# Two expert tiles computed during the second image's routing, a check moved into attention's tail, and the mambas' opening reordered

## The chip, the cores and the metric

The kernel runs on one core of a Trainium2 chip, in fp32 throughout. A core has engines with instruction streams of their own that synchronise by semaphores: TensorE (PE; its weight loads are shown as PEld), VectorE (DVE), ScalarE (ACT), GpSimd (POOL) and SyncE (SP). SP, ACT and POOL also issue DMAs. Each engine runs its instructions in the order in which they were written. The metric is the device time of one execution in microseconds (us), lower is better.

## The reference, cut to what matters

Four layers run over x of shape (2, 128, 56, 56): two images, 128 channels. Each layer adds its output to x, and each reads x after a group norm (32 groups per image).

```python
x = x + _L0(_gn(x))   # agent attention
x = x + _L1(_gn(x))   # 3x3 convolution
x = x + _L2(_gn(x))   # patch experts
x = x + _L3(_gn(x))   # two mambas, forward and backward, fused, layer norm

# layer 2: a token is a 2x2 patch of all channels: 2*784 = 1568 tokens of 512
logits = xp @ router_w                       # (1568, 8)
topv, topi = top_k(softmax(logits), 2); topv = topv / sum(topv)
for e in range(8):
    val, g = split(xp @ w1[e], 2)            # w1[e]: (512, 2048)
    out += gate[:, e:e+1] * ((val * sigmoid(g)) @ w2[e])   # w2[e]: (1024, 512)

# layer 3, for each row of the image (56 steps long)
xc = silu(conv_b + causal conv of 4 taps of (x @ in_w.T))
dt, B, C = split(xc @ xproj_w.T); dt = softplus(dt @ dt_w.T + dt_b)
h = exp(dt * A) * h + (dt * xc) * B          # 16 states per channel, scanned
y = (sum over states of h * C + xc * D) * silu(z)
```

The norm of an image needs the whole image, so a layer of image b can begin only when the layer before has ended for image b. The two images are independent of each other up to that.

## The kernel before

**Attention and the convolution.** Attention ends with a list `tail` of small stages that are put one by one before the pieces of the convolution of image 0 (`parts`, each a left or right half of the four groups of rows `GROUPS`). After the last group a check follows (L854 to L872): maxima and minima of attention's sums are compared with limits, and PE adds the findings of all partitions into `w_ps`, from which `wide` is set. `wide` chooses after this program whether a slower variant must run. Only then come the planes of image 1's convolution (L135, L947) and that convolution itself, the loop `conv(1)`, which yields after each group.

**Routing (`PatchExperts.route`).** `patches(b)` normalises image b into xq, computes the logits (l_ps, s_ps), takes the two best experts per token on DVE (L1122 to L1131), transposes the tokens (xt_ps, copied by ACT into one of four xt buffers) and writes them to DRAM (xd, seven DMAs of 224 KB on SP). `patches(0)` runs during `conv(1)`, `patches(1)` after it. Then, once for both images: the shares (L1156 to L1160, with an Exp on ACT), counts per expert (tot and pre on PE, a scan on DVE), the number of 128-slot tiles of each expert, the expert of each tile (`whose`), each token's slot, and 28 matmuls into `inv` (L1267) that turn "slot of each token" into "token and share of each slot". `whom` and `share` are copied from it (L1276, L1278). The scheduler also puts the preparation of the mambas' weights (`MambaWeights`: transposes tr_ps, copies L142, scalings L1471) into this stretch.

**Experts (`PatchExperts.run`).** At least 25 tiles (`fewest`) and up to 7 more in a Switch; 28 were run. For a tile j: SP loads w1 (4096 KB) and w2 (2048 KB) of the expert into one of two buffers each; POOL gathers the tile's 128 rows from xd (xr, an indirect DMA); `up` transposes them (xr_ps), DVE copies them (xs_c), 16 matmuls of 512 columns (each two records) give h_ps, ACT takes the sigmoid and DVE the product he; `down` of the tile before transposes he (he_ps) and multiplies by w2 (o_ps), scales by the share and writes to DRAM (os). Tile 0 waits for the gather, this for `whom`.

**The mambas' opening (`mamba_pair`).** `arrive(b)` is a generator that brings image b back: for each of seven pieces k0 to k6, POOL gathers two rows per token from os (g), DVE adds them, PE transposes the sum into y_ps, DVE adds it to x and takes statistics; last comes the norm (gn_ps twice, `ir_v`). `arrive(0)` runs alone. `arrive(1)` is called `second`, and runs in pieces beside the first block of image 0: an agenda of steps (conv, silu, low, step, error, log, softplus, weigh, send_steps, ...) is written out by hand, and after each step a number from a tuple says how many pieces of `second` are pulled. Every engine then keeps this order (`manual_schedule`). `send_steps` (L1795) copies dt and dt*u to the layout with two states per partition: for the first block per half m, eight DMAs of 112 KB for dtu on SP and eight for dt on ACT. After the opening the main loop begins: `decay` (L1807, exp on ACT), `push` (L1818, dBu on POOL), `scan` (L1840 on DVE), and the products with C (L1849 on DVE for most, L1846 on POOL for some), for which PE spreads C into c_ps (L1828).

Of the kernel before, what the change touches and what calls it, by code (L numbers as in the profile page):

```python
# [8 lines left out]
F32 = mybir.dt.float32  # L9
# [8 lines left out]
P = 128  # L18
# [390 lines left out]
def short_attention(net, wide, conv):  # L409
# [20 lines left out]
    with ExitStack() as ctx:  # L430
# [337 lines left out]
        with tc.manual_schedule(engines={E.PE, E.Activation, E.DVE}):  # L768
# [55 lines left out]
            for f in fetches:  # L824
                if f:
                    f()

# [7 lines left out]
                [deviations],  # L835
# [15 lines left out]


            bad = net.small.tile([P, 4], F32, name="bad", tag="bad")
            nc.vector.memset(bad, 0.0)  # L854
            worst = net.small.tile([P, 4], F32, name="worst", tag="worst")
            aflat = asum.rearrange("t b k h -> t (b k h)")
            for n, (v, op, cmp, limit) in enumerate(
                (
                    (ends[:, 0].rearrange("p b k -> p (b k)"), ALU.max, ALU.is_gt, 1e20),
                    (ends[:, 1].rearrange("p b k -> p (b k)"), ALU.min, ALU.is_lt, 1e-30),  # L860
                    (aflat, ALU.max, ALU.is_gt, 1e30),
                    (aflat, ALU.min, ALU.is_lt, 1e-20),
                )
            ):
                size = v.shape[0]
                nc.vector.tensor_reduce(worst[:size, n : n + 1], v, AX.X, op)
                nc.vector.tensor_single_scalar(bad[:size, n : n + 1], worst[:size, n : n + 1], limit, cmp)
            total = net.small.tile([P, 1], F32, name="bad_sum", tag="bad_sum")
            nc.vector.tensor_reduce(total, bad, AX.X, ALU.add)
            w_ps = bank("w_ps")  # L870
            nc.tensor.matmul(w_ps[0:1, 0:1], full[:, 0:1], total, start=True, stop=True)
            nc.vector.tensor_single_scalar(wide, w_ps[0:1, 0:1], 0.5, ALU.is_gt)  # L872
# [130 lines left out]
TILES = 32  # L1003


class PatchExperts:

# [14 lines left out]
    def route(self, dram, wpool, conv):  # L1022
# [9 lines left out]
        with tc.tile_pool(name="l2_route", bufs=1) as one, tc.tile_pool(  # L1032
            name="l2_route_ps", bufs=2, space=PSUM
        ) as ps:
            self.fewest = -(-2 * toks // SLOTS)
            none = one.tile([SLOTS, 512], F32, name="none")
# [38 lines left out]
            nc.gpsimd.tensor_scalar(floor, count_to[:, :most], float(SLOTS), 0.0, ALU.mult, ALU.add)  # L1075

# [5 lines left out]
            per = nt // NB  # L1082

            def patches(b):
                if b == 0:
                    self.xq = wpool.tile([P, 4, 2 * self.hidden], F32, name="xq", tag="w1")
                xq = self.xq
                mr = net.group_norm(b, ps, "tr")
                for q in range(4):
                    net.normed(  # L1090
                        xq[:, q, b * tok : (b + 1) * tok].rearrange("c (h w) -> c h w", w=half), self.place(b, q), mr
                    )
                lq = one.tile([P, tok], F32, name="lq", tag="lq")
                size = tok // 2
                for i in range(2):
                    l_ps = ps.tile([P, 512], F32, name="l_ps", tag="tr")
                    for q in range(4):
                        nc.tensor.matmul(
                            l_ps[32 * q : 32 * q + 32, :size],
                            rw[:, q, :],  # L1100
                            xq[:, q, b * tok + i * size : b * tok + (i + 1) * size],
                            start=True,
                            stop=True,
                        )
                    nc.scalar.copy(lq[:, i * size : (i + 1) * size], l_ps[:, :size])
                s_ps = ps.tile([P, 512], F32, name="s_ps", tag="tr")
# [16 lines left out]
                for n in range(2):  # L1123
# [6 lines left out]
                    if n == 0:  # L1130
# [7 lines left out]
                        )  # L1138
                for t in range(b * per, (b + 1) * per):
                    tp = ps.tile([P, 512], F32, name="xt_ps", tag="tr")  # L1140
                    for q in range(4):
                        nc.tensor.transpose(tp[:T, q * P : (q + 1) * P], xq[:, q, t * T : (t + 1) * T], net.ident)
                    xt = one.tile([T, 512], F32, name="xt", tag="xt", bufs=4)
                    nc.scalar.copy(xt, tp[:T, :])
                    nc.sync.dma_start(self.xd[t * T : (t + 1) * T, :], xt)

            for _ in conv(0):
                pass
            for k, _ in enumerate(conv(1)):
                if k == 0:  # L1150
                    patches(0)
            patches(1)


            share = [one.tile([T, nt], F32, name=f"share{n}") for n in range(2)]
            nc.vector.tensor_sub(share[1], tops[1], tops[0])  # L1156
            nc.scalar.activation(share[1], share[1], AF.Exp)
            nc.vector.tensor_scalar_add(share[0], share[1], 1.0)
            nc.vector.reciprocal(share[0], share[0])
            nc.vector.tensor_mul(share[1], share[1], share[0])  # L1160


            both = one.tile(shape, F32, name="both")
            nc.vector.tensor_add(both, hots[0], hots[1])
            flat = both.rearrange("t n e -> t (n e)")
            tot = ps.tile([P, 512], F32, name="tot", tag="tr")
            nc.tensor.matmul(tot[:, : nt * experts], every, flat, start=True, stop=True)
            pre = ps.tile([P, 512], F32, name="pre", tag="tr")
            nc.tensor.matmul(pre[:T, : nt * experts], before, flat, start=True, stop=True)
            by_e = one.tile([P, experts, nt], F32, name="by_e")  # L1170
            nc.vector.tensor_copy(by_e, tot[:, : nt * experts].rearrange("p (n e) -> p e n", e=experts))
            upto = one.tile([P, experts, nt], F32, name="upto")
            nc.vector.tensor_tensor_scan(
                upto.rearrange("p e n -> p (e n)"),
                step.rearrange("p e n -> p (e n)"),
                by_e.rearrange("p e n -> p (e n)"),
                0.0,
                ALU.mult,
                ALU.add,
            )  # L1180

            over = one.tile([P, experts, most], F32, name="over")
            nc.vector.tensor_tensor(
                over,
                upto[:, :, nt - 1 : nt].to_broadcast([P, experts, most]),
                floor.unsqueeze(1).to_broadcast([P, experts, most]),
                ALU.is_gt,
            )
            tiles = one.tile([P, experts], F32, name="tiles")
            nc.vector.tensor_reduce(tiles, over, AX.X, ALU.add)  # L1190
            ends = one.tile([P, experts], F32, name="ends")
            nc.vector.tensor_tensor_scan(ends, every_e(net, one, experts), tiles, 0.0, ALU.mult, ALU.add)

            more = keep.tile([1, 1], I32, name="more")
            nc.vector.tensor_scalar_add(more, ends[0:1, experts - 1 : experts], -float(self.fewest))
            self.more = more
# [933 lines left out]
```

## Time and profile before

| | |
|---|---|
| median of three runs | 3127.28 us (3126.38 to 3134.36) |
| the profiled execution | 3131.49 us |
| its span in the trace | 3129.8 us |
| mean granted TensorE clock | 0.931 |
| busy: PE, DVE, ACT, POOL | 2836.3, 2229.0, 1758.0, 1495.6 us |
| attention's scores (L617) | 40.1 to 888.4 us |
| convolutions (L971), from | 894.5 us |
| routing's end (whom, L1276) | 1023.5 us |
| experts' last output (L1353) | 1678.9 us |
| first scan of the mambas (L1840) | 1757.1 us |
| w1, w2: issue to landing (median) | 19.4, 10.2 us |

A line of a timeline gives the start in us from the span's start, the length, engine, line, operation, output and inputs with their shapes and the number of instructions merged, and in brackets the engine's idle time before it with what ended it. An fp32 matmul leaves two records. "ACTq" and "SPq" are DMA issues.

### The profile page before, as it was taken

What the parts mean: (1) busy time and instruction counts of PE and PEld (TensorE: products, weight loads), DVE (VectorE), ACT (ScalarE), POOL (GpSimd) and SP (SyncE); (2) the same over time, 40 slices, a digit from 0 to 9 for tenths busy, and PEclk for the clock granted to TensorE, in tenths of its full rate; (3) what the DMA queues carried; (4) which work ended last, traced back from release to release, by engine and by line L of the source; (5) the groups of instructions that cost most, each with busy time, mean ns of one, the idle gap of its engine ahead of it and who ended that gap; (6) DMA issues with size and microseconds to landing.
All of it is one profiled execution on the core that took longest, in us unless ns stands there. A gap on an engine that the chain in (4) does not pass through costs nothing. (4 is left out here: it accounts for less than half of the span.)

```text
span 3129.8 us, 34601 instructions
## 1 busy us (share of the span) xinstructions
PE 2836.3 (91%) x12964; PEld 1082.0 (35%) x12964; DVE 2229.0 (71%) x2033; ACT 1758.0 (56%) x2634; POOL 1495.6 (48%) x793
## 2 busy tenths in 40 slices
PE   7999999999988899999996789989899899899885
PEld 3333333332335444444443223333223333233321
DVE  5879999998886011111112689999999999999996
ACT  5778888887741011111110577776777776777764
POOL 3000100100521000000002589999999999999996
PEclk9999999999998899999997789999889998899987
DMA  1000000000011777777854553444434535444440
GB/s 54 1 1 1 1 1 1 1 1 1 1 38 53 311 308 302 301 310 292 319 194 161 104 110 77 93 92 102 90 84 86 114 81 107 90 85 91 93 101 8
DMA packets 133525, 333.64 MB, mean 107 GB/s; under 512 B 20228, under 2 KB 90724, under 8 KB 129748
## 3 DMA queue, kind: packets, MB, share of 16 engines
q1 hardware_dynamic: 111104, 303.96, 33.8%
q0 software_dynamic: 5136, 14.70, 1.4%
q10 hardware_dynamic: 17092, 12.53, 1.3%
q8 instruction: 106, 1.74, 0.2%
q14 instruction: 87, 0.71, 0.1%
HBM read 262.56 MB, written 17.20 MB: 89 GB/s over the span
## 5 line engine op out<-in xcount | busy, mean ns | idle before, releaser
L1818 POOL TENSOR_TENSOR dBu<-dtu,Bs 128x896 f32<-128x896 f32 x448 | 944.9, 2142 | 54.9 <-DVE h L1840 45.4
L1840 DVE TENSOR_TENSOR_SCAN h<-dA,dBu 128x896 f32<-128x896 f32 x448 | 879.1, 2007 | 51.3 <-ACT dA L1807 49.2
L620 ACT ACTIVATE ex<-sc 128x896 f32<-128x896 f32 (+1 forms) x700 | 602.6, 917 | 125.1 <-PE sc L617 113.8
L627 DVE TENSOR_TENSOR ex_sum<-ex_sum,ex 128x1792 f32<-128x1792 f32 (+1 forms) x238 | 492.5, 2069 | 35.3 <-ACT ex L620 21.3
L1860 PE MATMUL y<-h,both 128*64 128x448 f32 x1792 | 477.3, 635 | 13.7 <-POOL h L1846 12.6
L617 PE MATMUL sc<-q,k 32*128 32x448 f32 (+1 forms) x2800 | 403.8, 588 | 3.6 <-ACT ex L620 2.9
L1330 PE MATMUL h_ps<-w,xs_c 128*128 128x512 f32 x896 | 392.7, 596 | 11.8 <-issue 9.9
L1807 ACT ACTIVATE dA<-dt,f_A 128x448 f32<-128x448 f32 x448 | 284.4, 637 | 104.8 <-DVE h L1840 76.6
L635 PE MATMUL av<-ex,va 128*32 128x448 f32 (+1 forms) x2800 | 334.4, 552 | 0.1
L1849 DVE TENSOR_TENSOR h<-h,c_ps 128x1792 f32<-128x1792 f32 x154 | 311.3, 2022 | 26.8 <-PE c_ps L1828 12.3
L1334 DVE TENSOR_TENSOR he<-h_ps,sg 128x512 f32<-128x512 f32 x56 | 38.6, 691 | 397.7 <-PE h_ps L1330 374.9
L582 POOL TENSOR_TENSOR a_e<-a_e,a_inv 112x784 f32<-112x784 f32 x14 | 41.6, 2973 | 584.2 <-ACT ex L620 394.6
L1807 ACT ACTIVATE dA<-dt,b_A 128x448 f32<-128x448 f32 x448 | 283.7, 636 | 62.0 <-DVE h L1840 49.8
L1281 POOL DMA_INDIRECT xr<-xd,whom x28 | 28.0, 999 | 534.7 <-PE xr_ps L1320 494.7
L1846 POOL TENSOR_TENSOR h<-h,Cs 128x1792 f32<-128x1792 f32 x70 | 279.3, 3990 | 5.9 <-DVE h L1840 5.9
L1828 PE MATMUL c_ps<-low,ident 40*64 40x448 f32 x616 | 172.3, 640 | 91.5 <-DVE h L1849 69.3
L1330 PEld LDWEIGHTS h_ps<-w,xs_c 128*128 128x128 f32 x896 | 168.7, 191 | 220.3 <-issue 202.4
L1860 PEld LDWEIGHTS y<-h,both 128*64 128x64 f32 x1792 | 118.3, 152 | 320.6 <-issue 258.5
L617 PEld LDWEIGHTS sc<-q,k 32*128 32x128 f32 (+1 forms) x2800 | 137.9, 181 | 230.1 <-issue 132.5
L1351 PE MATMUL o_ps<-w,ht 128*128 128x512 f32 x448 | 198.7, 596 | 7.9 <-DMA w<-in_L_conv_w_dram 7.9
L1353 ACT ACTIVATE ot<-o_ps,share 128x512 f32<-128x512 f32 x28 | 19.2, 687 | 285.7 <-PE o_ps L1351 285.7
L1333 ACT ACTIVATE sg<-h_ps 128x512 f32<-128x512 f32 x56 | 33.4, 597 | 257.9 <-PE h_ps L1330 257.9
(333 smaller groups left out, 3067.5 us busy)
## 6 DMA issues: line engine op xcount, KB each, us to landing
w<-in_L_conv_w_dram SPq DMA_DIRECT2D x28, 4096.0 KB, 19.4
w<-in_L_conv_w_dram SPq DMA_DIRECT2D x28, 2048.0 KB, 10.2
Bs<-far SPq DMA_DIRECT2D x56, 896.0 KB, 10.7
dtu<-sp_u SPq DMA_DIRECT2D x108, 224.0 KB, 3.9
dt<-dt SPq DMA_DIRECT2D x108, 224.0 KB, 5.2
Cs<-far SPq DMA_DIRECT2D x140, 112.0 KB, 7.4
os<-ot ACTq DMA_DIRECT2D x28, 256.0 KB, 7.7
xd<-xt SPq DMA_DIRECT2D x14, 224.0 KB, 2.7
```

The lines of the kernel that those rows point to most:

```text
L617: nc.tensor.matmul(sc[:size, j, :BLK], self.m.k[rows, at : at + size], self.q[rows, :], start=True, stop=True)
L620: nc.scalar.activation(ex[:size, 2 * g : 2 * g + 2, :], sc[:size, :, :BLK], AF.Exp, scale=scale)
L627: nc.vector.tensor_add(self.total[g][:size], self.total[g][:size], ex[:size])
L635: nc.tensor.matmul(self.av[rows, :BLK], self.m.va[:size, i, rows], self.ex[i][:size, h, :], start=i == 0, stop=i == STEPS - 1,)
L1330: nc.tensor.matmul(h_ps, xc[:, q, :], w1[:, q, f0 : f0 + 512], start=q == 0, stop=q == 3)
L1351: nc.tensor.matmul(o_ps, ht[:, i, :], w2[:, i, :], start=i == 0, stop=i == nj - 1)
L1807: nc.scalar.activation(self.dA[u][:, r * BLK : (r + 1) * BLK], self.dt2[:, m, r, :], AF.Exp, scale=self.w.A[:, j, 2 * m + r : 2 * m + r + 1],)
L1818: nc.gpsimd.tensor_tensor(self.dBu[u], self.dtu2[:, m], self.B[:, j, :].unsqueeze(1).to_broadcast(shape), ALU.mult)
L1840: nc.vector.tensor_tensor_scan(hf, af, bf, 0.0, ALU.mult, ALU.add)
L1846: nc.gpsimd.tensor_tensor(h4, h4, c, ALU.mult)
L1849: nc.vector.tensor_tensor(h4, h4, c, ALU.mult)
L1860: nc.tensor.matmul(self.y[r * H : (r + 1) * H, m, :BLK], both, self.hc[j][:, m, r, :], start=False, stop=j == PAIRS - 1)
```

## The change

1. The check's DVE instructions become `judge`, its matmul `verdict`, and both are put into attention's tail.
2. `EARLY = 2` tiles are taken ahead. After `patches(0)`, `first_tiles` finds two tiles that are full with image 0's tokens (a copy of the routing for seven token groups, with 14 matmuls of four columns into inv_0), and `ahead` issues their weights and gathers. A tile's work is cut into stages (turn; four times four products; of the tile before: turn and two halves of o_ps). `patches(1)` and the rest of the routing are written in a fixed order for PE and ACT, with `go(n)` putting the next n stages in between: thirteen in all, those are both tiles' `up` and tile 0's `down`. Tile 0's sigmoids are held until the shares' Exp is done. The routing of all tokens counts the full tiles of image 0 first and the rest after, so that every tile of the first kind keeps its number. xq holds one image at a time (`room`), xt has two buffers instead of four; `inv` is built in four halves that share `room` with xq. The mambas' weights are prepared after the routing, and kept in the same `room`.
3. In the opening the tuple is another, and dt's eight DMAs of the first block are issued by POOL instead of ACT. In the order that results, dt's issues stand ahead of the last two pieces' gathers (k5, k6) on POOL, and the norm of image 1 and its two matmuls ahead of the backward conv on PE.

```diff
+            def judge():
+                bad = net.small.tile([P, 4], F32, name="bad", tag="bad")
...
+                nc.vector.tensor_reduce(total, bad, AX.X, ALU.add)
+                judged.append(total)
+            def verdict():
+                w_ps = bank("w_ps")
+                nc.tensor.matmul(w_ps[0:1, 0:1], full[:, 0:1], judged[0], start=True, stop=True)
+                nc.vector.tensor_single_scalar(wide, w_ps[0:1, 0:1], 0.5, ALU.is_gt)
...
-                [deviations],
+                [deviations, judge],
+                [],
+                [verdict],
...
             def patches(b):
-                if b == 0:
-                    self.xq = wpool.tile([P, 4, 2 * self.hidden], F32, name="xq", tag="w1")
+                go = self.go if b == 1 else lambda n: None
+                got = []
+                go(2)
+                for stage in net.norm_stages(b, ps, "o", got.append):
+                    fetch = stage()
+                    if fetch:
+                        fetch()
+                        go(1)
...
+                go(1)
+                s_ps = ps.tile([P, 512], F32, name="s_ps", tag="o")
...
+                shares(some)
+                if b == 1:
+                    held, self.held = self.held, None
+                    for stage in held:
+                        stage()
                 for t in range(b * per, (b + 1) * per):
...
-                    xt = one.tile([T, 512], F32, name="xt", tag="xt", bufs=4)
+                    xt = one.tile([T, 512], F32, name="xt", tag="xt", bufs=2)
                     nc.scalar.copy(xt, tp[:T, :])
                     nc.sync.dma_start(self.xd[t * T : (t + 1) * T, :], xt)
+                    if t % 4 == 1:
+                        go(1)
...
+            def first_tiles():
+                some = slice(0, per)
...
+                pre = counted(both, by_e, upto, steps)
...
+                nc.vector.tensor_scalar_min(self.whose_0, whose, float(experts - 1))
...
+                inv = ps.tile([P, 512], F32, name="inv_0", tag="o")
+                for n in range(2):
+                    hot = one.tile(here, F32, name="hot_0", tag="hot_0")
+                    nc.vector.tensor_copy(hot, hots[n][:, some, :])
+                    split(hot, slot, some, at)
+                    lq = one.tile([P, small_room], F32, name="lq", tag="lq")
+                    turned(inv[:, : 2 * EARLY], lq, n, some, EARLY, n == 0, n == 1)
+                self.whom_0 = keep.tile([P, EARLY], I32, name="whom_0")
+                nc.vector.tensor_copy(self.whom_0, inv[:, :EARLY])
...
                 if k == 0:
                     patches(0)
-            patches(1)
+                    first_tiles()
+                    self.ahead()
+            with tc.manual_schedule(engines={mybir.EngineType.PE, mybir.EngineType.Activation}):
+                patches(1)
...
+                pre = counted(both, by_e, upto, step)
...
+                self.go(2)
...
+                for n in range(2):
+                    at_n = one.tile([T, nt], F32, name=f"at{n}")
+                    split(hots[n], slot, slice(0, nt), at_n)
...
+                    for b in range(NB):
+                        self.go(1 if self.stages else 0)
+                        turned(
                             inv[:, : 2 * TILES],
+                            room[:, b * size : (b + 1) * size],
...
+        def ahead():
+            self.stages, self.held = [], []
+            for j in range(EARLY):
+                e = expert(j)
+                self.stages += step(j, e, up_weights(e), gather(j))
+    def later(self, stage):
+        if self.held is None:
+            stage()
+        else:
+            self.held.append(stage)
+    def go(self, n):
+        for _ in range(n):
+            self.stages.pop(0)()
...
-        for j in range(self.fewest):
+        for j in range(EARLY, self.fewest):
             e = expert(j)
-            w1, w2 = up_weights(e), down_weights(e)
...
+            tile(j, e, up_weights(e), gather(j))
...
+        room = one.tile([P, N], F32, name="weights", tag="room")
...
-                for to, src, queue in ((self.dtu2, self.dtu, nc.sync), (self.dt2, self.dt, nc.sync if m is None else nc.scalar)):
+                for to, src, queue in ((self.dtu2, self.dtu, nc.sync), (self.dt2, self.dt, nc.sync if m is None else nc.gpsimd)):
...
-                for _ in range((0, 0, 0, 0, 2, 1, 2, 1, 2, 0, 0, 0, 0, 0, 1, 1, 1)[step - first] if step - first < 17 else 1):
+                for _ in range((0, 0, 0, 2, 0, 0, 1, 0, 0, 1, 1, 0, 3, 1, 1, 1)[step - first] if step - first < 16 else 1):
                     next(second, None)
...
-                    experts.route(dram, wpool, convolved)
-                    wts = MambaWeights(net, one, nat, bank)
...
+                    experts.begin(wpool, work, ps)
+                    room = one.tile([P, 4 * experts.tok], F32, name="room", tag="room")
+                    experts.route(dram, work, ps, room, convolved)
+                    with tc.tile_pool(name="l3_nat", bufs=2) as nat:
+                        wts = MambaWeights(net, one, nat, bank)
+                    experts.run()
```

## The prediction

> **What bounds the kernel now.** I read the page's 40 slices first. TensorE (PE) is at 9 or 8 tenths in most slices; the change works in two places where it is not: around 30% (the experts' start) and 54 to 57% of the span (the mambas' opening). The windows of the experts' start follow; columns: stretch, its length, busy time of PE, PEld, DVE, ACT, POOL, then granted clock, DMA share, GB/s.
>
> ```profile
> 983.00:1011.00 28.00, 18.30 (x101) 11.99 (x100) 23.90 (x104) 5.94 (x14) 1.31 (x2) 0.81 0.18 59
> 1011.00:1024.00 13.00, 12.18 (x56) 12.02 (x56) 4.27 (x10) 0.00 (x0) 0.04 (x1) 0.50 0.71 283
> 1024.00:1034.76 10.76, 1.99 (x8) 1.62 (x9) 0.69 (x1) 0.00 (x0) 5.09 (x5) 0.50 1.03 388
> 1034.76:1073.70 38.94, 38.13 (x98) 17.38 (x97) 4.84 (x7) 5.02 (x8) 1.55 (x2) 0.96 0.67 271
> ```
>
> From 983 to 1034.76 PE does small work and waits; two tiles' products (38.9 us) come after that. PE's timeline of it (start, length, idle time before in brackets):
>
> ```profile
> 935.45 0.19 PE L871 MATMUL w_ps<-bad_sum,full 128*1 128x1 f32 x2 [5.63 <-DVE bad_sum L869]
> ...
> 969.07 13.73 PE L971 MATMUL conv_ps<-planes,cwt 128*128 128x448 f32 x48
> ...
> 991.16 3.60 PE L1098 MATMUL l_ps<-xq,rw 128*32 128x392 f32 x16
> ...
> 1011.26 12.18 PE L1267 MATMUL inv<-room 112*128 112x64 f32 x56 [5.18 <-DVE tile_f L1242]
> 1031.36 1.09 PE L1320 MATMUL xr_ps<-ident,xr 128*128 128x128 f32 x4 [7.92 <-DMA xr<-xd,whom]
> ...
> 1034.76 15.55 PE L1330 MATMUL h_ps<-w,xs_c 128*128 128x512 f32 x32
> ...
> 1053.38 13.90 PE L1330 MATMUL h_ps<-w,xs_c 128*128 128x512 f32 x32
> 1067.11 5.31 PE L1351 MATMUL o_ps<-w,ht 128*128 128x512 f32 x12
> ...
> 1073.70 13.97 PE L1330 MATMUL h_ps<-w,xs_c 128*128 128x512 f32 x32 [0.39 <-issue]
> ```
>
> The third tile's products start at 1073.70 and one tile then takes 22.54 us (1073.70 to 1096.24): whatever start the third tile has is handed on to the end. For the opening, the timelines of DVE, ACT and PE:
>
> ```profile
> 1756.07 0.16 DVE L66 TENSOR_SCALAR ir_v<-gn_ps 128x1 f32<-128x1 f32 x1 [7.38 <-PE gn_ps L116]
> 1757.09 2.02 DVE L1840 TENSOR_TENSOR_SCAN h<-dA,dBu 128x896 f32<-128x896 f32 x1 [0.86 <-ACT dA L1807]
> ...
> 1769.32 2.02 DVE L1849 TENSOR_TENSOR h<-h,c_ps 128x1792 f32<-128x1792 f32 x1
> ```
> ```profile
> 1743.51 2.55 ACTq L1795 DMA_DIRECT2D dt<-dt  x4
> 1746.10 0.53 ACT L1773 COPY dt<-sp_ps 128x448 f32<-128x448 f32 x1 [3.46 <-issue]
> ```
> ```profile
> 1747.90 8.01 PE L1690 MATMUL conv_ps<-pad,b_conv_t 128*128 128x448 f32 x16
> ...
> 1766.61 1.76 PE L1828 MATMUL c_ps<-low,ident 40*64 40x448 f32 x4
> ```
>
> The first scan waits for the second image's norm (`ir_v`), and that for `gn_ps`, which PE runs behind the backward conv's 8.01 us. The first product with C (L1849) starts as c_ps (1766.61) and the fourth scan end together.
>
> **Part 1, the check (`judge`).** Its ten DVE instructions and `w_ps` stand between the last statistics (932.87) and the next planes (L135, 935.92). Beside attention's tail they cost nothing as long as the conv's matmuls cover them (PE busy 29.82 of 900 to 933); without cover 1.85 us, their sum. Gain 2.4 us (0.5 to 2.4).
>
> **Part 2, two tiles ahead.** I work out when the third tile's products can start. Conv(1) ended at 982.8. It starts 2.4 earlier, and takes on tot and pre (0.45 each before), 14 `inv` matmuls of four columns (nearest row: 14 records of s_ps, seven matmuls, in 1.45 at clock 0.97, so 0.2 each: 2.9), and about 1 us of waits, since xt has two buffers and an xd takes 2.7 to land (0 to 3): end 985.2. Then the list of tokens (0.2), the gather's issue (1.0) and landing, with 6 MB of weights in flight behind it: xr's rows give 2.7 (xd, idle queue) to 7.4 (the first gather, at DMA share 1.03). I take 991.5. On POOL the two gathers, which wait for that list, stand ahead of conv(1)'s last sums (L991/L992), so image 1's statistics come at about 988; SP has the xd copies of image 0 ahead of w1, which costs nothing while those land by 973. PE runs in its written order, so image 1's norm and routing stand behind tile 0's gather and w1:
> - tile 0 and 1: xr and its copy 2.0 and 0.6, products 15.4 and 13.7;
> - norm 0.9, l_ps 3.6, s_ps 1.6, seven xt 3.7, tot and pre 0.9;
> - 28 `inv`: the row is 12.18, at clock 0.50; s_ps at clock 0.97 is 0.207 a matmul, so 5.8. Now 512-column products lie between the groups, as from 1034.76 on, where the clock was 0.96: I take 6.1 (5.8 to 12.2);
> - down(0): he 1.2, o_ps 7.0.
>
> Sum 56.7. The Trainium skill, "TensorE: Matmul & The Clock Gate", Part 1, says that the clock is halved by default and released by some 3.4 us of sustained work; here PE was busy for 12.18 of 13 us and the clock stayed 0.50, so the rule alone would not have given the row. By the rule the sum is as above; if `inv` cannot raise the clock, as in the row, it is 6.1 us worse.
>
> Idle time inside: the Exp of the shares, a table load (1.28 us in the opening) and two sigmoids (0.6 each) come ahead of the xt copies on ACT, behind twelve DVE selections of 0.2: xt waits 4.5; two xt buffers instead of four make PE wait for two landings (0.58 + 0.3 + 2.7 each, less 3.2 of work): 4; tot for `both`: 1. Together 9.5 (3 to 15). `inv` ends at 1057.7, whom at 1058.1, the gather (1.0, landing 7.3 to 8.0) at 1066.3, xr and he to products 1.4: 1067.7. Left is the mambas' weights: 34 copies and 16 scalings of 0.28 on DVE, 14 us which before lay beside the routing (983 to 1007). Now they start at 1058; the gather's wait hides 8, and transposes between tile 2's products cost PE 3 to 6. Effective start 1072.5 against 1073.70. **Gain 1.2, judge included** (from a gain of 9: few stalls and a quick gather, to a loss of 7: `inv` at half clock, as many stalls).
>
> The steady tiles and the Switch keep their instructions; the number of tiles does not grow, since each full tile taken early is one less later.
>
> **Part 3, the opening.** dt's eight copies go from ACT to POOL. ACT's copy of sp_ps (m = 1) no longer stands behind four issues: 1746.10 becomes about 1744.3 (PE's last sp_ps ends there), and with fewer y_ps pieces between, up to 5 earlier. But POOL then has, in order: memset, four issues, memset, four issues, and only then the gathers of the last two patch tiles (k5, k6), which before had been issued by 1729.5. POOL's direct issues at the program's start took 0.53 to 0.82; at 0.65 and a first memset at 1738 to 1743.4, the issues end by 1743.5 to 1748.8. The last of four gathers (one each 1.28) begins 3.8 later and lands after 3.4 (median of `g`). Add 0.9, y_ps 1.3, additions 1.0, statistics 0.7, aggregate to `ir_v` 2.0: 5.9. So `ir_v` at 1756.6 to 1761.9 against 1756.07, and the first scan 0.5 to 5.8 late. PE's backward conv (8.0, now after `gn_ps`) ends at 1764.5 to 1769.8 instead of 1755.9; xc, table load and silu 2.9, low 3.2, its copy 0.5, gate 1.9, c_ps 1.8: first L1849 at 1775 to 1780, 6 to 11 late. Waited on behind it are DVE's next scans and ACT's dt for the backward half. DVE's idle time up to 1810 (1.09, 2.84, 4.77, 1.24, 1.87, 2.63) could absorb some; it hangs on the same chain, so I let 6 through. **Loss 6 us** (0 to 11; a gain of 3 if POOL is quick, since dBu's first product ends at 1752.7 and only `ir_v` held the first scan back).
>
> The Trainium skill, "DMA: Bandwidth & Descriptors", Specifications, gives the GpSimd path a first byte at about 1 us and the sync/scalar path 0.6, a rule against this move; ACT's rows here are 4.0 us to landing, POOL's for plain copies are not shown. By the rule the sum would be 0.4 worse.
>
> **Sum.** -1.2 + 6 = +4.8 on the profiled execution, 3131.49 (span 3129.8 and 1.7 around it): 3136.3. That run lies 4.2 above the median of the runs, 3127.28; against that: **3132**.
>
> **Rivals.**
> - *The opening absorbs its delay, and the routing's stalls are small* (faster). For: DVE idles 14.4 us just behind the first L1849; ACT is freed of 5.2 us of issues. Against: those waits name ACT's dt and PE's c_ps. Experts -9, opening -3: 3115. Chance 0.17.
> - *POOL's queue decides the opening* (slower). POOL runs dBu and the gathers in order; if its issues take 0.8 and its gathers land late (5.4 at most before), L1849 is 11 late and all of it is kept; with the xt stalls at their upper end (+4 to +7) 3143. It decides from 9.4 us in sum. For: POOL's dBu is already what follows. Chance 0.28.
> - *The early tiles do not run early*: w1 lands late (19.4 us is the median to landing, in steady state) and image 1's norm stands behind it on PE. Landing at 995 rather than 990 costs 4: 3136. Inside the forecast's range.
>
> **How the numbers follow.** Forecast (little change) 0.55, faster 0.17, slower 0.28. A measurement of this kernel can tell about 0.3% (9.4 us) from no change, so these are also the three chances. The likeliest case alone spans 3123 to 3137; the bounds together -9 to +18; leaving a tenth out on either side, 3119 to 3143.
>
> **What would show it.** `w_ps` gone from before the planes; tile 0's h_ps near 993; `inv` in four groups, ending at 1057 and at a clock near 0.95; h_ps of the third tile between 1068 and 1077 with tr_ps among it; gathers g of k5 and k6 behind dt's issues on POOL; `ir_v` at 1757 or later and L1849 6 or more behind its place relative to the end of the experts. I am wrong if the experts' gain exceeds 10, if the first L1849 is not late, or if the tiles' 22.54 us has changed.

## The result, and the profile after

| | before | after |
|---|---|---|
| median, lowest and highest of 14 runs each | 3127.32 us (3122.20 to 3134.36) | 3137.48 us (3132.06 to 3148.23) |
| profiled execution, its span | 3131.49, 3129.8 us | 3145.05, 3143.3 us |
| mean granted clock | 0.931 | 0.927 |

The ratio after to before is 1.0035, with a 95% interval of 1.0023 to 1.0047: slower by 10.2 us, just beyond the 0.3% that can be told from no change. The forecast was 3132 us with a range of 3119 to 3143. The range held the time; the likeliest case, 3123 to 3137, did not. The two profiled executions lie 4.2 and 7.6 us above the medians of their kernels, so the traces differ by more than the medians do.

I compared the two traces at the same events. Each time is the start of the instruction, and the last row is the end of the span:

| event | before | after minus before |
|---|---|---|
| attention's last score | 888.8 us | +1.4 |
| first matmul of the convolutions | 894.5 | +2.1 |
| first matmul of conv(1) | 938.5 | +2.1 |
| first products of the fourth tile | 1096.2 | +1.6 |
| experts' last o_ps | 1678.3 | +1.1 |
| opening's pad | 1710.9 | +1.2 |
| first scan | 1757.1 | +6.7 |
| fifth scan | 1773.0 | +13.3 |
| last scan | 3100.8 | +12.7 |
| end | 3129.8 | +13.6 |

The first 2.1 us arise before the convolutions, in code that the change leaves alone: in the traces of this case the first matmul of the convolutions starts anywhere from 892.7 to 899.5 us. From there to the experts' end the change gains about 1 us (2.1 becomes 1.1); the opening costs 12.2 us, from pad to fifth scan, and of that 11.5 are left at the last scan.

Three timelines of the kernel after show the opening, of POOL, DVE and PE in this order; the columns are those of the timelines before.

```profile
1736.76 0.11 POOL L1984 MEMSET dt<- 128x8 f32 x1 [12.08 <-DVE sp_u L1980]
1737.31 2.16 POOL L1995 DMA_DIRECT2D dt<-dt  x4 [0.43 <-POOL dt L1984]
1739.49 0.11 POOL L1984 MEMSET dt<- 128x8 f32 x1
1739.99 2.06 POOL L1995 DMA_DIRECT2D dt<-dt  x4 [0.40 <-POOL dt L1984]
1745.16 1.04 POOL L1419 DMA_INDIRECT g<-os,at_i  x1 [3.11 <-DMA dt<-dt]
...
1749.12 0.99 POOL L1419 DMA_INDIRECT g<-os,at_i  x1 [0.31 <-issue]
```
```profile
1752.57 2.23 DVE L1601 TENSOR_TENSOR g<-g,g 112x512 f32<-112x512 f32 x1 [13.14 <-DMA g<-os,at_i]
...
1762.79 0.16 DVE L66 TENSOR_SCALAR ir_v<-gn_ps 128x1 f32<-128x1 f32 x1 [0.74 <-PE gn_ps L116]
1763.81 2.02 DVE L2040 TENSOR_TENSOR_SCAN h<-dA,dBu 128x896 f32<-128x896 f32 x1 [0.86 <-ACT dA L2007]
...
1779.42 2.02 DVE L2040 TENSOR_TENSOR_SCAN h<-dA,dBu 128x896 f32<-128x896 f32 x1 [7.20 <-ACT dA L2007]
1781.76 2.02 DVE L2049 TENSOR_TENSOR h<-h,c_ps 128x1792 f32<-128x1792 f32 x1 [0.32 <-PE c_ps L2028]
```
```profile
1754.94 0.99 PE L1604 MATMUL y_ps<-ident,g 112*128 112x112 f32 x4 [16.74 <-DVE g L1601]
...
1762.61 9.07 PE L1890 MATMUL conv_ps<-pad,weights 128*128 128x448 f32 x16
...
1779.96 1.76 PE L2028 MATMUL c_ps<-low,ident 40*64 40x448 f32 x4
```

In the kernel before, POOL had issued all gathers ahead of its first memset, which waited for DVE:

```profile
1724.55 0.98 POOL L1281 DMA_INDIRECT g<-os,at_i  x1 [0.30 <-PE y_ps L1408]
...
1728.50 0.98 POOL L1281 DMA_INDIRECT g<-os,at_i  x1 [0.30 <-issue]
1743.36 0.11 POOL L1784 MEMSET dt<- 128x8 f32 x1 [13.89 <-DVE sp_u L1780]
```

In the change POOL's four gathers of the last two pieces stand behind both memsets on dt and eight issues. DVE waits 13.14 us for them and PE 16.74. The norm of image 1 follows, and only behind its matmuls PE runs the backward conv, which before began at 1747.90 and now at 1762.61. What follows from that conv is late: ACT's silu (L1899, L2071), the fourth scan's dA behind it on ACT (DVE waits 7.20), c_ps and the first product with C (1769.32 before, 1781.76 now).

In the experts, PE's timeline of the kernel after answers to the one shown of before:

```profile
931.66 0.19 PE L852 MATMUL w_ps<-bad_sum,full 128*1 128x1 f32 x2 [0.91 <-DVE bad_sum L847]
932.28 2.51 PE L979 MATMUL conv_ps<-planes,cwt 128*128 128x224 f32 x12 [0.43 <-DVE x L996]
...
996.10 1.12 PE L1465 MATMUL xr_ps<-ident,xr 128*128 128x128 f32 x4 [5.31 <-DMA xr<-xd,whom]
...
1023.99 1.10 PE L1168 MATMUL xt_ps<-ident,room 128*112 128x128 f32 x4 [4.53 <-ACT xt L1170]
...
1056.95 1.67 PE L1246 MATMUL inv<-room 112*128 112x64 f32 x14
...
1066.45 0.69 PE L1465 MATMUL xr_ps<-ident,xr 128*128 128x128 f32 x2 [4.31 <-DMA xr<-xd,whom]
...
1073.76 1.12 PE L1475 MATMUL h_ps<-w,xs_c 128*128 128x512 f32 x2 [0.27 <-DVE xs_c L1467]
```

PE now has products to do from 998 on, where before it ran the routing and waited, from 1011 to 1034 us at half clock. But the gather of the third tile can only be issued when `inv` ends at 1058.6. PE has a few small transposes for that time (tr_ps) and then waits 4.31 us; behind xr_ps more transposes for the mambas' weights come, 7.3 us until the first product, and others between the third tile's products. The fourth tile starts at 1097.88 against 1096.24.

### The profile page after: what moved, and what is told of

It reads as the page before. It is cut to its first block, busy times and chain, and to the rows that moved or that the text cites. A ratio compares the mean times of both kernels' runs of the same rounds, so it can differ in the third digit from the quotient of the medians.

```text
span 3143.3 us, 34651 instructions
## 1 busy us (share of the span) xinstructions
PE 2842.2 (90%) x12996; PEld 1080.0 (34%) x12996; DVE 2246.2 (71%) x2096; ACT 1758.2 (56%) x2635; POOL 1500.0 (48%) x804
## 5 line engine op out<-in xcount | busy, mean ns | idle before, releaser
L2060 PE MATMUL y<-h,weights 128*64 128x448 f32 x1792 | 476.4, 633 | 12.2 <-POOL h L2046 11.2
L1475 PE MATMUL h_ps<-w,xs_c 128*128 128x512 f32 x896 | 395.9, 598 | 10.9 <-issue 10.3
L2049 DVE TENSOR_TENSOR h<-h,c_ps 128x1792 f32<-128x1792 f32 x154 | 311.3, 2021 | 28.0 <-PE c_ps L2028 13.6
L2060 PEld LDWEIGHTS y<-h,weights 128*64 128x64 f32 x1792 | 118.1, 152 | 320.9 <-issue 257.7
L1890 PE MATMUL conv_ps<-pad,weights 128*128 128x448 f32 x448 | 186.0, 563 | 3.6 <-ACT pad L1797 2.4
## 6 DMA issues: line engine op xcount, KB each, us to landing
w<-in_L_conv_w_dram SPq DMA_DIRECT2D x28, 2048.0 KB, 10.2
Cs<-far SPq DMA_DIRECT2D x140, 112.0 KB, 10.3
```

The costliest lines, as they stand in the source:

```text
L1475: nc.tensor.matmul(has["h"][:, n, :], has["xc"][:, q, :], w1[:, q, f0 : f0 + 512], start=q == 0, stop=q == 3)
L2049: nc.vector.tensor_tensor(h4, h4, c, ALU.mult)
L2060: nc.tensor.matmul(self.y[r * H : (r + 1) * H, m, :BLK], both, self.hc[j][:, m, r, :], start=False, stop=j == PAIRS - 1)
```

## The experiments

Medians are over the runs of each, with the ratio to before measured on the same chip and its 95% interval. The ratio is not that of the two medians: in before_again, the same code on both sides, the medians differ by 2.8 us and the ratio is 1.0001. Traces are compared over the stretch that a change touches, since single executions of one kernel differ by some microseconds elsewhere.

**opening_undone**: the change with the old opening, so its experts and its check alone.

```diff
-  ... nc.sync if m is None else nc.gpsimd
+  ... nc.sync if m is None else nc.scalar
-  (0, 0, 0, 2, 0, 0, 1, 0, 0, 1, 1, 0, 3, 1, 1, 1)[step - first] if step - first < 16 else 1
+  (0, 0, 0, 0, 2, 1, 2, 1, 2, 0, 0, 0, 0, 0, 1, 1, 1)[step - first] if step - first < 17 else 1
```

> The changed kernel with the opening of before (the old tuple, dt's copies on ACT). Theory (the opening alone loses 12.6 us, the experts and the check together gain 1.4, the 2.1 us up to attention's end is noise): ratio to before 0.9995, some 3126 us; third tile within 1 us of where it is in the changed kernel relative to attention's end, first L1849-kind product 12 us after the first scan as before. Rival (the new pools, the shared weights room or the experts' order also slow the mambas or the experts): at least half of the loss stays, 3132 us or more.

Measured: 3129.45 us, ratio 1.0019 (1.0009 to 1.0028). In the trace the first convolution to the last o_ps is 0.1 us shorter than before, and pad to fifth scan 0.7 shorter. So the loss of 12.2 sits in the opening. The median's 5 us over before (3124.15 in this set of runs) is found in no stage up to the fifth scan; I come back to it below.

**queue_back**: the change with dt's eight issues on ACT again, the new tuple kept.

```diff
-  ... nc.sync if m is None else nc.gpsimd
+  ... nc.sync if m is None else nc.scalar
```

> The changed kernel with dt's copies back on ACT, the new tuple kept. Theory (POOL's queue is the cause: eight issues and the wait of the next gather for a landed dt copy): the gathers of k5 and k6 go out some 8 us earlier, the norm's ir_v comes 6 us earlier or more, and of the 12.6 us at least 6 come back: 3126 to 3132 us. Rival (the order of pieces alone is the cause, with the backward conv behind the norm): within 3 us of the changed kernel, 3134 to 3138 us.

Measured (five runs): 3141.05 us, ratio 1.0049 (1.0036 to 1.0062); pad to fifth scan 12.2 longer than before. My theory that POOL's queue makes the delay fell. POOL's timeline of this kernel says why:

```profile
1742.42 0.11 POOL L1984 MEMSET dt<- 128x8 f32 x1 [14.78 <-DVE sp_u L1980]
1746.36 0.11 POOL L1984 MEMSET dt<- 128x8 f32 x1 [3.82 <-DVE sp_u L1980]
1747.16 0.99 POOL L1419 DMA_INDIRECT g<-os,at_i  x1 [0.69 <-issue]
...
1751.02 0.98 POOL L1419 DMA_INDIRECT g<-os,at_i  x1 [0.30 <-issue]
```

No dt issue stands there, and the gathers are as late: they stand behind the two memsets, and these wait for DVE's sp_u. A memset of 0.11 us holds the four gathers back: counted from each kernel's own pad, the first of them starts at 32.9 us here and at 13.6 in the kernel before.

**tuple_back**: the converse, the change with the old tuple and dt on POOL (the second line of the diff of opening_undone).

> The changed kernel with the old tuple, dt's copies still on POOL. Theory (POOL's issues hurt only because gathers stand behind them; with the old tuple all gathers are out before): no loss, 3123 to 3128 us, and ACT free of 5 us of issues gives up to 3. Rival (copies issued by POOL are slow by themselves, in issue, landing or by holding dBu back): the loss stays by half or more, 3132 us or above.

Measured: 3127.14 us, ratio 1.0009 (1.0000 to 1.0019); pad to fifth scan 1.5 us shorter than before. POOL's timeline here:

```profile
1726.43 0.99 POOL L1419 DMA_INDIRECT g<-os,at_i  x1 [0.30 <-issue]
1741.20 0.11 POOL L1984 MEMSET dt<- 128x8 f32 x1 [13.79 <-DVE sp_u L1980]
1741.75 2.15 POOL L1995 DMA_DIRECT2D dt<-dt  x4 [0.43 <-POOL dt L1984]
1743.89 0.13 POOL L1984 MEMSET dt<- 128x8 f32 x1
1744.32 2.06 POOL L1995 DMA_DIRECT2D dt<-dt  x4 [0.29 <-POOL dt L1984]
```

All gathers are out before the first memset, and the issues on POOL cost nothing that shows. The gain of up to 3 us does not show in the time either.

**opening_alone**: the kernel before with the new opening, both edits of it.

```diff
-  ... nc.sync if m is None else nc.scalar
+  ... nc.sync if m is None else nc.gpsimd
-  (0, 0, 0, 0, 2, 1, 2, 1, 2, 0, 0, 0, 0, 0, 1, 1, 1)[step - first] if step - first < 17 else 1
+  (0, 0, 0, 2, 0, 0, 1, 0, 0, 1, 1, 0, 3, 1, 1, 1)[step - first] if step - first < 16 else 1
```

> The kernel of before with the new opening alone (new tuple, dt's copies on POOL), experts and check as before. Theory (the loss is the opening's and adds to anything): 12 to 13 us slower, ratio 1.0040, some 3139 us. Rival (the opening only loses because the experts leave it a different state): ratio below 1.002.

Measured (six runs): 3134.25 us, ratio 1.0031 (1.0019 to 1.0042); pad to fifth scan 12.1 longer. The opening alone makes the loss, 1.0031 against the change's 1.0035.

**before_again**: the kernel before once more, for the spread of a trace.

> The kernel of before, unchanged, for the spread of the measurement and for a second trace. All theories: ratio 1.0000 within 0.0010. If the experts of the changed kernel are neutral (as the traces so far say, -1 to 0 us from the convolution to the experts' end), this trace is some 5 us shorter than the first one of before (3129.8) in stages that the change leaves alone, and that explains why the changed kernel with the old opening was timed 1.0019; if the experts cost 5 us, this trace shows them 5 us shorter from the convolution to the experts' end than the trace of the changed kernel with the old opening.

Measured: 3125.08 us, ratio 1.0001 (0.9988 to 1.0014). Its span is 3120.5 us against 3129.8 in the first trace of the same code. Of these 9.3 us, 8.3 lie between the fifth scan and the end, in part as single blocks of the main loop that take 2.2 us longer in one trace than in the other. Differences of that size in the main loop of one trace mean nothing here.

**pool_queue_alone**: the kernel before with dt's issues on POOL and nothing else (the first line of the diff of opening_alone).

> Before with dt's eight copies on POOL and nothing else. Theory (the queue is a small gain where no gather stands behind it): 1 to 4 us faster, ratio 0.9988 to 0.9997, first scan 3 us earlier. Rival (issues on POOL cost as such): slower by 2 us or more.

Measured: 3125.20 us, ratio 0.9995 (0.9986 to 1.0004). Pad to fifth scan is 2.1 us shorter than in the first trace of before, 1.1 than in the second. With tuple_back this clears the queue a second time.

**conv_first**: if lateness of the backward conv is what counts, an opening with that conv as early as the old order allows should win. On top of dt on POOL, image 1's norm is pulled right after its last piece, and the backward conv and its silu are booked four steps earlier.

```diff
-  book(at + 17, lambda b=b: b.conv(0))
-  book(at + 17, lambda b=b: b.conv(1), tag="c")
-  book(at + 19, lambda b=b: silu(b, None))
+  book(at + 13, lambda b=b: b.conv(0))
+  book(at + 13, lambda b=b: b.conv(1), tag="c")
+  book(at + 15, lambda b=b: silu(b, None))
-  (0, 0, 0, 0, 2, 1, 2, 1, 2, 0, 0, 0, 0, 0, 1, 1, 1)[step - first] if step - first < 17 else 1
+  (0, 0, 0, 0, 2, 1, 2, 1, 2, 1, 1, 1)[step - first] if step - first < 12 else 1
```

> Before with dt on POOL, the second image's norm pulled right after its last piece (three stages earlier), and the backward conv four steps earlier, behind the last sp_ps. Theory (what sets the first products with C is when PE can begin the backward conv and what stands before ir_v): conv starts 3 us earlier, ir_v 10 us earlier, first scan at dBu's first end (some 6 us earlier than before), first product with C 4 to 7 us earlier, and 3 to 7 us stay to the end: ratio 0.9978 to 0.9990. Rival (the opening is bound elsewhere, the early gain is lost by the fifth scan): within 2 us of the kernel with the queue alone.

Measured: 3123.88 us, ratio 0.9986 (0.9976 to 0.9996), by the medians 4 us faster. `ir_v` comes at 1742.14 and the conv at 1741.97. Counted from each kernel's own pad, the first product with C starts at 54.1 us, against 58.4 in the kernel before and 57.4 in pool_queue_alone; but pad to fifth scan takes 58.7 us, against 62.0 and 60.0. Over pool_queue_alone that is 1.3 us, as in the medians, and the two intervals overlap: the rival, within 2 us of the queue alone, is not excluded, and what the early conv gains is in part lost again by the fifth scan.

**conv_first_experts**: the change with that opening.

> The changed kernel with that same improved opening. Theory (experts neutral): same as the run before it within 2 us, so faster than before by 3 to 7 us. Rival (the new experts and check cost 4 to 6 us): 4 to 6 us slower than the run before it, about level with before.

Measured: 3124.66 us, ratio 0.9985 (0.9974 to 0.9997). The early tiles and the check together are worth nothing that shows, 0.9985 against 0.9986. Together with the stretches of the traces this speaks against a real loss in opening_undone. Its 1.0019 keeps an interval off 1 all the same, and I have not found where it comes from. Part of it may be the baseline: the kernel before, on that same chip, had a median of 3124.15 us in the set of opening_undone and of 3127.13 in the later set of judge_alone.

**pieces_before_memset**: the change with the tuple's 3 moved up two steps, so that the last pieces' gathers are issued ahead of the first memset; the backward conv stays behind the norm.

```diff
-  (0, 0, 0, 2, 0, 0, 1, 0, 0, 1, 1, 0, 3, 1, 1, 1)
+  (0, 0, 0, 2, 0, 0, 1, 0, 0, 1, 4, 0, 0, 1, 1, 1)
```

> The changed kernel with the three pieces pulled together taken two steps earlier (the tuple's 3 moves from its thirteenth to its eleventh place), so that POOL's gathers of k5 and k6 stand ahead of the two memsets on dt, which wait for DVE's products, and ahead of dt's copies. Everything else as changed. Theory (the opening's loss is that wait and the queue behind it, not the norm standing before the backward conv): gathers by 1735, ir_v at 1752 or before, and 9 to 13 of the 12 us come back: ratio 0.9990 to 1.0010. Rival (the loss is the backward conv standing behind the norm): at least half of the loss stays, 1.0015 or more.

Measured: 3126.11 us, ratio 0.9994 (0.9983 to 1.0004). Two lines of POOL's timeline and two of PE's:

```profile
1728.74 0.99 POOL L1419 DMA_INDIRECT g<-os,at_i  x1 [0.31 <-issue]
1743.02 0.11 POOL L1984 MEMSET dt<- 128x8 f32 x1 [13.29 <-DVE sp_u L1980]
...
1747.24 0.56 PE L116 MATMUL gn_ps<-gn_q,group 128*128 128x1 f32 x2 [0.79 <-DVE gn_q L110]
1747.66 7.70 PE L1890 MATMUL conv_ps<-pad,weights 128*128 128x448 f32 x16
```

Gathers are out by 1729.73, `ir_v` comes at 1747.83, the backward conv at 1747.66, still behind the norm, and the first product with C at 1765.59. All of the loss is back with this one move, so the order of norm and conv on PE was not what cost; late gathers were.

**judge_alone**: the kernel before with the check in attention's tail, edit 1 of the change by itself.

```diff
-                [deviations],
+                [deviations, judge],
+                [],
+                [verdict],
```

> Before with the check moved into attention's tail and nothing else. Prediction's reason: 2.4 us faster. What the trace of the changed kernel showed instead: the first image's last conv group ends 2.8 us later relative to its first, and the second image's conv begins where it began, so 0 us (within 0.7 in the trace from the first conv to the second), ratio within 0.0010 of 1.

Measured: 3128.26 us, ratio 1.0005 (0.9996 to 1.0014). A gain of 2.4 us would be 0.9992, outside the interval. In the trace the stretch from the first convolution to conv(1) is 41.2 us, against 44.0 and 43.6 in the two traces of before; from the first convolution to the fourth tile 1.3 and 0.6 us of it are left. The gain is there at its place: the stretch to conv(1) takes 43.6 to 44.0 us in all five traces with the old check and the old routing. It does not show in the time, and at the fourth tile it can't be told, since those five differ there by 3.6 us (198.1 to 201.7).

**routing_first**: the change with the opening of conv_first, and the two halves of o_ps of tile 0's `down` put behind the last `inv` instead of between its four groups (the turn of he stays between), so that `whom` comes sooner and PE has products while the third tile's gather lands.

```diff
                     for b in range(NB):
-                        self.go(1 if self.stages else 0)
+                        self.go(1 if b == 0 else 0)
...
                 nc.vector.tensor_copy(self.share, inv[:, TILES : 2 * TILES])
+                self.go(len(self.stages))
```

> The changed kernel with the improved opening of before and the two halves of tile 0's o_ps behind the routing's last inv instead of between its groups. Theory (PE's written order holds whom back, the tiles' work ahead gives back what the routing loses): whom 3 to 5 us earlier, the third tile's xr 3 us earlier, the fourth tile's products 2 to 4 us earlier than with the same opening and the old places, ratio 0.9965 to 0.9985. Rival (DVE's preparation of inv sets whom): whom within 1 us of where it was, no change.

Measured: 3117.56 us, ratio 0.9968 (0.9957 to 0.9978): 10 us faster than the kernel before, of which conv_first_experts, without the move of o_ps, already had 0.0015 of 0.0032; and some 20 us faster than the change. PE's timeline of this kernel:

```profile
1038.78 3.24 PE L1246 MATMUL inv<-room 112*128 112x64 f32 x28
1041.86 1.04 PE L1499 MATMUL he_ps<-ident,he 128*128 128x128 f32 x8
1044.58 5.54 PE L1246 MATMUL inv<-room 112*128 112x64 f32 x28 [1.69 <-DVE room L1242]
1049.91 8.23 PE L1510 MATMUL o_ps<-w,ht 128*128 128x512 f32 x16
1057.98 0.27 PE L141 MATMUL tr_ps<-ident,f_scaled 128*128 128x128 f32 x1
1058.09 0.60 PE L1466 MATMUL xr_ps<-ident,xr 128*128 128x128 f32 x4
...
1086.79 3.67 PE L1476 MATMUL h_ps<-w,xs_c 128*128 128x512 f32 x8 [0.39 <-issue]
```

Counted from the first convolution, `inv` ends at 157.4 us, against 162.0 in the change and 160.6 in conv_first_experts. The gather of the third tile lands under the 8.23 us of o_ps, and xr_ps follows with no wait, where the change waited 4.31. Then the third tile's products start 1.4 us after xr_ps, at a granted clock of 1.00; in the change it is 7.3 us at 0.63, and in conv_first_experts 7.5 at 0.50, with transposes for the mambas' weights in between. Some of this comes back, since more of these transposes now lie in the third tile, which takes 27.3 us instead of 24.1 and 26.3. From the first convolution to the fourth tile it takes 194.1 us, against 200.9 in before_again, 201.2 in the change and 198.1 to 202.4 in all other traces. Against conv_first_experts that is 8.3 us less, more than the 2 to 4 expected; the ratios of the two, measured on two chips, have intervals that just touch. The idea of the two early tiles is sound; what hid its gain was where tile 0's o_ps stood.

## Why the prediction was right, and where it was wrong

**The opening: the term was mis-sized, 6 against 12.2.** The chain up to the first product with C went as worked out, at its upper end or just beyond. Taken against the 1.2 us by which the opening started late, `ir_v` came at 1761.6 (I had 1756.6 to 1761.9), the conv ended at 1770.5 (1764.5 to 1769.8; it took 9.07 us, not 8.0), and the first L1849 at 1780.6, 11.3 late (6 to 11). The step that failed is "DVE's idle time up to 1810 (1.09, 2.84, 4.77, 1.24, 1.87, 2.63) could absorb some; it hangs on the same chain, so I let 6 through". Here are those waits in DVE's timeline of the kernel after:

```profile
1785.77 0.62 DVE L1962 SCALAR_TENSOR_TENSOR sp_e<-dt_ps,sp_e 128x448 f32<-128x448 f32 x1 [1.99 <-ACT dt_ps L1956]
1797.14 0.62 DVE L1962 SCALAR_TENSOR_TENSOR sp_e<-dt_ps,sp_e 128x448 f32<-128x448 f32 x1 [2.84 <-ACT dt_ps L1956]
1808.29 2.02 DVE L2049 TENSOR_TENSOR h<-h,c_ps 128x1792 f32<-128x1792 f32 x1 [4.77 <-PE c_ps L2028]
1813.48 2.02 DVE L2040 TENSOR_TENSOR_SCAN h<-dA,dBu 128x896 f32<-128x896 f32 x1 [1.23 <-ACT dA L2007]
1817.37 2.02 DVE L2049 TENSOR_TENSOR h<-h,c_ps 128x1792 f32<-128x1792 f32 x1 [1.87 <-PE c_ps L2028]
1822.02 7.76 DVE L2040 TENSOR_TENSOR_SCAN h<-dA,dBu 128x896 f32<-128x896 f32 x4 [2.62 <-ACT dA L2007]
```

Two of the same waits in the kernel before:

```profile
1783.80 0.62 DVE L1762 SCALAR_TENSOR_TENSOR sp_e<-dt_ps,sp_e 128x448 f32<-128x448 f32 x1 [2.84 <-ACT dt_ps L1756]
1794.96 2.02 DVE L1849 TENSOR_TENSOR h<-h,c_ps 128x1792 f32<-128x1792 f32 x1 [4.77 <-PE c_ps L1828]
```

All six are there again, 13.3 us later; the first grew by 0.90, and the others agree to a hundredth. They are waits for the backward half's own chain, which begins at the late conv, so they move with it and absorb nothing. Had the whole 11 gone into the sum, the forecast would have been 3137 us.

**The place was right, the reason half.** My sum began at the first memset and put the delay down to the eight issues behind it. They do stand ahead in the change, but without them it is the same: counted from each kernel's own pad, the second memset comes at 27.4 us in the change and at 32.1 in queue_back, the first late gather at 33.1 and 32.9. With dt on POOL the issues (2.16 and 2.06 us) and the wait of 3.11 fill what is otherwise spent waiting for sp_u. What decides is that the gathers stand behind the memsets at all. The rival "POOL's queue decides the opening" had the size (all 11 kept) but not the cause: the issues took 0.52 to 0.54 us each, and not 0.65 to 0.8. That the first late gather came at 1744.0, less the 1.2 us, and so inside my 1743.5 to 1748.8, was luck: the first memset came at 1735.6, before my 1738 to 1743.4, and the wait of 3.11, which I did not have, made up for it. I also wrote that POOL's plain copies are not shown to landing; at the program's start they are, with 2.3 to 10.3 us, and in pool_queue_alone the dt copies take a median of 4.7 from POOL, against 4.0 from ACT before.

**The early tiles: right in size.** Forecast 1.2 us of gain, judge included; the traces give 0.5 up to the fourth tile and 1.0 up to the experts' end, both within the spread of that stretch, and the medians nothing that can be told from zero. Of its steps, less the 2.1 us that attention brought: `inv` took 6.7 us in all (6.1 forecast, 12.18 before), at full clock; `whom` was done at 1056.7 (1058.1 forecast); gather 0 came at 994.0 (991.5). The third tile's products began at 1073.76, with tr_ps among them, inside 1068 to 1077, and the tiles kept their 22.55 us (1097.88 to 1120.43).

**The check: its gap closed, its gain not kept.** Before, 3.05 us lay between the last statistics and the next planes (932.87 to 935.92); in the change it is 0.54, as forecast. But the statistics themselves are late. Two lines of DVE's timeline of the kernel after:

```profile
928.46 0.16 DVE L69 TENSOR_TENSOR ir_t<-ir_v,gn_rstd 128x1 f32<-128x1 f32 x1 [2.25 <-ACT gn_rstd L68]
...
937.37 0.62 DVE L88 BATCH_NORM_STATS2 st<-x 128x6 f32<-128x448 f32 x1
```

Less the 2.1 us of attention, 937.37 is 2.4 late, and conv(1) starts at the same distance as before. Ahead of it DVE waits 2.25 us in attention's last norm for ACT, and the check's ten instructions come between that norm and the conv's additions. My claim that beside the tail "they cost nothing as long as the conv's matmuls cover them" looked at PE alone; the conv's results also need DVE. But in judge_alone this delay is absent, so the check does not make it alone. ACT's timelines show a difference that comes with edit 2, first in the kernel after, then in the one before:

```profile
924.76 2.73 ACTq L1698 DMA_DIRECT2D f_A<-in_L_conv_f_Alog_dram  x3
927.54 0.20 ACT L67 ACTIVATE ir_t<-ir_v 128x1 f32<-128x1 f32 x1 [2.82 <-DMA f_A<-in_L_conv_f_Alog_dram]
...
923.74 0.20 ACT L67 ACTIVATE ir_t<-ir_v 128x1 f32<-128x1 f32 x1 [1.05 <-DMA f_dw<-in_L_conv_f_dt_w_dram]
```

In the change ACT issues loads of the mambas' A in a row ahead of that norm, where before and in judge_alone other loads stand; and DVE scales A (L1700, 1.03 us) among the check's instructions. Counted from the first convolution and against judge_alone, the conv's last addition on DVE ahead of that norm is about 1 us late, L69 is 1.8 late and the conv's next addition 2.5. So the loads and the scaling can account for part of the delay at most; no run moves them by themselves, and the cause stays open.

**What would show it** listed `w_ps` before the planes, `inv` in four groups ending near 1057, gathers behind dt's issues, `ir_v` at 1757 or later, L1849 6 or more late: all five came. Tile 0's h_ps, forecast near 993, came at 995.9 less the 2.1 us. The forecast of no change that can be told was missed by 0.8 us, 10.2 against a bound of 9.4.

Two things were not tried: more than two xt buffers, and weights in memory of their own. Why the median of opening_undone lies 5 us above before stays open.

## What to carry to other kernels

An idle stretch absorbs a delay only if what it waits for does not itself hang on what is late: follow the releaser's chain back to the moved work before any idle time is taken off the loss. On an engine that runs in order, a tiny instruction that waits (here a memset of 0.11 us) is as dear as everything written behind it, so gathers that nothing holds back belong ahead of it. And when work is taken early to fill idle time, keep some of it for the wait that comes next: the same two tiles gave nothing that shows with o_ps between the `inv` groups, and, by the traces, 4 to 8 us with it behind them.

## What the runs showed of the hardware

- **A plain copy can hold up a gather on POOL.** The first gather after eight dt copies waited 3.11 us in the change and 2.01 in opening_alone, with the landing of a dt copy as releaser. The gather reads none of that data. The trace of before has the same pattern at its start: POOL issues eight copies, and then the ninth waits 2.65 us for the first to land, the tenth 1.98 for the second and the eleventh 0.51 for the third. That looks like eight in flight at most; no run varies the number, and whether the chip or the program sets it is not shown.
- **DVE's additions slow down beside POOL's.** The 112x512 addition of two gathered tiles (L1601) took 0.69 us in queue_back, where POOL was idle, and 1.46 to 2.23 in the change beside dBu; in queue_back two one-column operations of the norm took 1.98 and 2.00 us beside dBu, against 0.16 and 0.22 in the change. The Trainium skill, "GPSIMD Engine Reference", Specifications, says that GpSimd's SBUF interfaces are shared with VectorE, with contention where a DVE instruction has two SBUF inputs; these rows agree. The price, 0.8 to 1.8 us an instruction beside dBu's 2.1, comes on top for delayed gathers when they run into dBu.
- **The same matmuls at two clocks, a few us apart.** In routing_first the first half of `inv` took 3.24 us at a granted clock of 1.00, and the second, behind a wait of 1.69 us, 5.54 at 0.57. In the change, with he_ps or half of o_ps between the groups, all four ran at a granted clock of 1.00 (1.67 us each).
